# Attention scores from three digit products on two row tiles instead of plain float32, with two row buffers instead of four

## The chip, the cores and the metric

The kernel runs on one core of a Trainium2 chip. The time is the device time of one execution in microseconds (us). The kernel before takes 2467.72 us, the median of three runs (2467.32 to 2469.74).

## The reference

The input x holds 64 batch elements of 256 rows and 512 columns in float32, and adj is a 256 x 256 matrix of zeros and ones. Two layers follow each other, each with a residual and a layer norm:

```
# layer 0: attention with 8 heads of 64, masked by adj
q, k, v = x @ Wq + bq, x @ Wk + bk, x @ Wv + bv      # split into heads
scores = einsum('bqhd,bkhd->bhqk', q, k) / sqrt(64) + (1 - adj) * -1e9
out = einsum('bhqk,bkhd->bqhd', softmax(scores), v)
x = layernorm(x + out @ Wo + bo)
# layer 1
x = layernorm(x + einsum('nm,bmd->bnd', adj, x) @ weight + bias)
```

## The kernel before

The batch is worked through in 32 pairs of elements. A pair has 512 rows, so that a transposed block of its rows (xT) is a tile of 128 x 512, and every matrix product comes in blocks of 128 x 512 outputs in one PSUM bank.

**Digits.** A large product in float32 is made of three products of digits in the type F32R. `split_high` and `split_rest` (weights), `x_high` and `rest` (rows), `o_high` and `set_high` (the other left sides) cut a tile into a high digit (ScalarE, a copy with a scale to F32R), a low rest and a mixed third part `diff` (two VectorE instructions, lines 262 and 263). For weights a fourth instruction rescales the low part on ScalarE. `product` then runs 12 matmuls per block, three for each of four slices of the contraction: low, high and diff in this order (line 312). The scores are the exception: `scores` multiplies K and Q as plain float32 (line 383), 64 rows of contraction per head, with two heads at a time on the upper and lower half of the array (the two row tiles).

**Stages.** In the middle of the run each pair w takes one call of `first(w)` and one of `second(w)`, which interleave three pairs: q = w - 1, w, and n = w + 1.

- `first`: `values(q, 1)` (softmax sums and attention times V of head group 1 of the earlier pair), `scores(w, 0)`, four v blocks, q2, k2, q3, k3 of pair w (head group 1), then four o blocks (times Wo) of pair q.
- `second`: `values(w, 0)`, `scores(w, 1)`, then q0, k0, q1, k1 of the next pair n with an `adj_x` (adj times x) after each, then four l blocks (times the second layer's weight) of pair q.

Between the blocks stand the tasks of ScalarE (ACT) and VectorE (DVE). The order on PE, DVE and ACT is the order in which the program is written (`manual_schedule`), and each of these engines takes its instructions strictly in that order: one that waits holds up all behind it. Only the queues of SyncE (SP) and GpSimd (POOL) are ordered by the framework.

**What the steps below touch.**

- `scores` (lines 374 to 388) has four groups, (b, kc). Each fills two PSUM tiles of the pool `ps_at`, one per row tile, and ScalarE empties them with two Exp instructions (line 387). The pool has five buffers and `values` takes three of them just before: one for the softmax sums `zc` and two for `vc`, which ScalarE copies out (lines 343 and 356). So the sixth score tile waits for the first Exp, the seventh for the second and the eighth for the third.
- `load_x(p, i)` (lines 75 to 80) fetches block i of pair p's rows by four DMAs of 64 KB on SP's queue, in pieces of 128 bytes. `x_t` (lines 248 to 252) transposes it on DVE (line 251) and asks for the same block of the pair after: there are four buffers, so a block is asked for a whole pair ahead of its use. In `first`, `x_t(n, 0)` and `x_t(n, 1)` stand among the v blocks, `x_t(n, 2)` and `x_t(n, 3)` among the o blocks.
- The weights of a stage, 3 MB of digits, are fetched by POOL (line 114) into a ring of two stages when a stage's last block is done (`stage_end`).
- The layer norm of a pair's l result runs `mean` (DVE), `squared` (ACT, line 424), `inverse` (DVE and a power on POOL, line 430), `less` (DVE, line 435), `normed` (ACT, line 441). `with_b1` adds the bias to a residual tile (line 406, 128 x 1024 on DVE). `masked` and `summed` (lines 392 and 397) are the mask times the exponentials and their sums.
- A block's PSUM tile `mm` comes from a pool of three buffers, which are handed out in turn to blocks and `adj_x` alike.

Of the kernel before, what the change touches and what calls it, by code (L numbers as in the profile page):

```python
# [35 lines left out]
def fast(tc, x, adj, wq, bq, wk, bk, wv, bv, wo, bo, w1, b1, out):  # L36
# [34 lines left out]
    RAW, SCRATCH, W = {}, {}, {}  # L71

    def load_x(p, i):

        if p < NP:
            t = XC[p, i] = four.tile([P, D], F32, name="x")
            for q in range(4):
                nc.sync.dma_start(t[q * 32:(q + 1) * 32].rearrange("i (m j) -> i m j", j=32), xb[p, i, q])  # L80

# [79 lines left out]
    nc.gpsimd.memset(ones, 1.0)  # L161
    rows0 = []
    for i in range(4):
        t = four.tile([P, D], F32, name="o")
        nc.sync.dma_start(t, xc[0, i // 2, i % 2])
        rows0.append(t)
    for which, w in (("q", wq), ("k", wk)):
# [10 lines left out]
        nc.scalar.dma_start(RAW[which][:, :, HF:], w.rearrange("(c p) e -> p c e", p=P)[:, :, HF:])  # L178
    adj_s = two.tile([P, NC, N], F32, name="vc")
    nc.sync.dma_start(adj_s, adj.rearrange("(c p) m -> p c m", p=P))  # L180
    for i in range(4):
        load_x(1, i)
    for k in range(DC):
        if k % 2 == 0:
# [63 lines left out]
    def x_t(p, k):  # L248
        if p < NP:
            XF[p, k] = two.tile([P, D], F32, name="xT")  # L250
            nc.vector.transpose(XF[p, k], XC.pop((p, k)))
            load_x(p + 1, k)

    def x_high(p, k):
        if p < NP:
# [50 lines left out]
    def product(name, p, j):  # L306
        pm = ps_mm.tile([P, D], F32, name="mm")
        pairs = [operands(name, p, j, k) for k in range(DC)]
        n = len(pairs[0])
        for i in range(n):  # L310
            for k in range(DC):
                nc.tensor.matmul(pm, *pairs[k][i], start=i == 0 and k == 0, stop=i == n - 1 and k == DC - 1)  # L312
        scale = RHO if n == 3 else 1.0
        b, c = divmod(j, 2)
        if name in "ol":
            r = R[p][b][:, c]
            if c == 0:
                ST[p, name, b] = two.tile([P, 2], F32, name="sums")
            nc.vector.scalar_tensor_tensor(r, pm, scale, r, op0=OP.mult, op1=OP.add, accum_out=ST[p, name, b][:, c:c + 1])  # L319
        elif name == "v":  # L320
            if c == 0:
                V[p, b] = two.tile([P, NC, D], F32, name="v")
            nc.scalar.activation(V[p, b][:, c], pm, AF.Copy, scale=scale)
        else:
            T, bias = (K, bk_s) if name == "k" else (Q, bq_s)
            if c == 0:
                T[p, b] = two.tile([P, 2, 2, N], F32, name=name + "T")
            nc.scalar.activation(T[p, b][:, c].rearrange("p b i -> p (b i)"), pm, AF.Identity, bias=bias[:, j:j + 1], scale=scale)  # L328

    def values(p, g, between=()):
# [34 lines left out]
        total = acc.rearrange("p b j -> p (b j)")  # L367
        nc.gpsimd.tensor_tensor(total, total, seen, op=OP.add)
        for b in range(2):
            O[p, b, g] = four.tile([P, 2, N], F32, name="o")  # L370
            nc.vector.tensor_tensor(O[p, b, g], vc[b], rs[:, b, None].to_broadcast([P, 2, N]), op=OP.mult)

    def scores(p, g):
        if not 0 <= p < NP:
            return
        for b in range(2):
            for kc in range(NC):

                sc = [ps_at.tile([P, 2, N], F32, name="at") for s in range(2)]
                for a in range(2):  # L380
                    for s in range(2):
                        r = slice(s * HD, (s + 1) * HD)
                        nc.tensor.matmul(sc[s][:, a, :], K[p, g][r, a, b, kc * P:(kc + 1) * P], Q[p, g][r, a, b, :],  # L383
                                         start=True, stop=True)
                e = E[p, g, b, kc] = one.tile([P, 2, 2, N], F32, name=f"e{2 * b + kc}")
                for s in range(2):
                    nc.scalar.activation(e[:, s], sc[s], AF.Exp, scale=qscale)  # L387

    def masked(p, g, b, kc):
        if 0 <= p < NP:  # L390
# [8 lines left out]
    def masks(p, g, b):  # L399
        return [(masked, p, g, b, 0), (masked, p, g, b, 1), (summed, p, g, b)]  # L400
# [12 lines left out]

    def mean(p, name, b):
        if 0 <= p < NP:
            t = LN[p, name, b] = [small.tile([P, 2], F32, name=n) for n in ("mean", "squares", "rstd", "less")]
# [89 lines left out]

    def second(w, more=([], [], [])):
        q, n = w - 1, w + 1
        values(w, 0, [(squared, q, "o", 2), (squared, q, "o", 3), (hl_low, q, 0, 0), (hl_low, q, 0, 1)])
        scores(w, 1)  # L510
        masks0, masks1 = masks(w, 1, 0), masks(w, 1, 1)
        do((inverse, q, "o", 1), (with_b1, q, 0), more[0],
           (block, "q", n, 0), (less, q, "o", 1), (normed, q, "o", 2), (normed, q, "o", 3),
           (adj_x, q, 0, 0), (hl_high, q, 1, 0), (hl_low, q, 1, 0), masks0[:1], more[1],
           (block, "k", n, 0), (adj_x, q, 0, 1), (hl_high, q, 1, 1), masks0[1:2], (hl_low, q, 1, 1), masks0[2:], more[2],
           (block, "q", n, 1), (adj_x, q, 1, 0), masks1[:1],
           (block, "k", n, 1), (stage_end, n), (with_b1, q, 1), (adj_x, q, 1, 1), masks1[1:],
           (block, "l", q, 0), (block, "l", q, 1), (mean, q, "l", 0), (squared, q, "l", 0), (squared, q, "l", 1),
           (o_high, w, 0, 0), (inverse, q, "l", 0), (o_rest, w, 0, 0),
           (block, "l", q, 2), (less, q, "l", 0), (normed, q, "l", 0), (normed, q, "l", 1),  # L520
           (block, "l", q, 3), (mean, q, "l", 1), (o_high, w, 1, 0), (o_rest, w, 1, 0), (stage_end, q))
# [6 lines left out]
    def start():  # L528
        do(*((x_first, i) for i in range(4)), *((x_high, 0, i) for i in range(4)))
        v, qk1, qk0 = (pairs_of(ring_high, ring_rest, *stage) for stage in STAGES[:3])  # L530
        do((block, "q", 0, 0), (x_rest, 0, 0), (x_rest, 0, 1), v[0], (block, "k", 0, 0), (x_rest, 0, 2), v[1],
           (block, "q", 0, 1), (x_rest, 0, 3), v[2], qk1[0], (block, "k", 0, 1), (adj_t,), (square_adj,))
        scores(0, 0)
        do(qk1[1], masks(0, 0, 0), (block, "v", 0, 0), qk1[2], (x_t, 1, 0), (x_t, 1, 1),
           (block, "v", 0, 1), (x_high, 1, 0), (x_high, 1, 1), (x_rest, 1, 0), (x_rest, 1, 1), (x_t, 1, 2), (x_t, 1, 3),
           (block, "v", 0, 2), masks(0, 0, 1), (x_high, 1, 2), (x_high, 1, 3),
           (block, "v", 0, 3), (stage_end, 0), (x_rest, 1, 2), (x_rest, 1, 3),
           (block, "q", 0, 2), (block, "k", 0, 2), qk0[0], (block, "q", 0, 3), qk0[1], (block, "k", 0, 3), qk0[2],
           (stage_end, 0), (load_r, 0), (load_l,))
        values(0, 0)  # L540
        scores(0, 1)
        do((bv_wo,), (block, "q", 1, 0), masks(0, 1, 0), (block, "k", 1, 0), masks(0, 1, 1),
           (block, "q", 1, 1), (o_high, 0, 0, 0), (o_rest, 0, 0, 0),
           (block, "k", 1, 1), (stage_end, 0), (o_high, 0, 1, 0), (o_rest, 0, 1, 0))

    def last():

# [228 lines left out]
```

## Time and profile before

| what | value |
|---|---|
| median of three runs | 2467.72 us |
| time of the profiled execution | 2468.09 us |
| its span | 2466.3 us |
| PE busy | 2432.4 us (99%) |
| DVE busy | 1675.3 us (68%) |
| ACT busy | 1299.3 us (53%) |
| POOL busy | 429.7 us (17%) |
| mean granted TensorE clock | 0.996 |
| moved by DMA | 603.23 MB, 245 GB/s |

In the lines of the profile an instruction is named by line, engine, operation and tiles, as out<-in; then come the count, the busy time of the group, the mean duration in ns, and the idle time of the engine just before, with what ended it. PEld is the weight load of TensorE, which overlaps the matmul before. A float32 matmul of the program appears as two matmuls in the trace. In a timeline the first column is the start and the second the length of a run of like instructions, in us.

### The profile page before, as it was taken

The numbers are of one execution on the slowest core, as the hardware profiler recorded it, in microseconds if no ns is written. First come the engines' busy times: TensorE is split into PE (matmuls) and PEld (weight loads), VectorE is DVE, ScalarE is ACT, GpSimd is POOL, SyncE is SP. The second block draws the span as 40 slices with busy tenths as digits, with TensorE's granted clock in tenths as the row PEclk, the third lists the DMA queues.
The fourth block names the chain that finished last, engine by engine and source line by source line (L and its number), as shares of the span: only waits on it lengthen the run. The fifth ranks groups of instructions, "written<-read, shape, count | busy, mean of one in ns | idle before, by whom it ended". The sixth has DMA issues, their size and how long they took to land.

```text
span 2466.3 us, 39819 instructions
## 1 busy us (share of the span) xinstructions
PE 2432.4 (99%) x15886; PEld 1933.6 (78%) x15886; DVE 1675.3 (68%) x2807; ACT 1299.3 (53%) x2418; POOL 429.7 (17%) x720
## 2 busy tenths in 40 slices
PE   8989999999999999999999999999999999999997
PEld 6777877877878778778778787787787787877875
DVE  7766667676666766676766667666767666676665
ACT  6555454554554554545545545545455455455454
POOL 0011111111111111111111111111111111111110
PEclk9999999999999999999999999999999999999998
DMA  8868777678786687776787866878767878768650
GB/s 262 275 224 266 248 256 269 231 231 267 244 293 238 223 267 248 256 269 229 232 267 243 296 237 221 268 248 256 268 230 232 267 243 294 238 222 269 230 188 35
DMA packets 370701, 603.23 MB, mean 245 GB/s; under 512 B 272848, under 2 KB 275152, under 8 KB 310224
## 3 DMA queue, kind: packets, MB, share of 16 engines
q0 software_dynamic: 65664, 478.18, 52.1%
q1 hardware_dynamic: 302736, 120.37, 21.3%
q8 instruction: 126, 2.06, 0.3%
q10 hardware_dynamic: 2112, 2.10, 0.2%
q14 instruction: 63, 0.52, 0.1%
HBM read 551.29 MB, written 49.28 MB: 244 GB/s over the span
## 4 chain that ended last, share of the span: by engine, by line
PE 97%; DVE 2%; ACT 1%; DMA 0%; issue 0%; POOL 0%; SPq 0%; POOLq 0%; ACTq 0%; DVEq 0%
PE mm L312 71%; PE at L383 10%; PE at L353 9%; PE mm L468 5%; PE at L341 3%; DVE e L392 0%; DMA o<-in_x_dram 0%; ACT r L441 0%; DVE sl L262 0%; ACT waste L424 0%; DVE hl L458 0%; DVE sd L263 0%; PE mm L227 0%; DVE r L319 0%; DVE wr L128 0%; DVE wr L127 0%
## 5 line engine op out<-in xcount | busy, mean ns | idle before, releaser
L319 DVE SCALAR_TENSOR_TENSOR r<-mm,r 128x512 f32<-128x512 f32 x256 | 173.4, 686 | 411.4 <-PE mm L312 409.3
L392 DVE TENSOR_TENSOR e<-e,adjT 128x1024 f32<-128x1024 f32 x256 | 306.2, 1218 | 1.8 <-ACT e L387 1.7
L424 ACT ACTIVATE waste<-r,mean 128x512 bf16<-128x512 f32 x256 | 184.2, 720 | 226.7 <-DVE mean L417 222.6
L312 PE MATMUL mm<-wr,sl 128*128 128x512 f32 x1024 | 277.3, 392 | 4.0 <-DVE sl L262 4.0
L312 PE MATMUL mm<-wr,sh 128*128 128x512 f32 x1024 | 275.2, 390 | 0.0
L312 PE MATMUL mm<-wr,sd 128*128 128x512 f32 x1024 | 274.8, 390 | 0.0
L312 PE MATMUL mm<-low,wr 128*128 128x512 f32 x992 | 271.7, 395 | 0.0
L387 ACT ACTIVATE e<-at 128x512 f32<-128x512 f32 x512 | 257.6, 627 | 20.8 <-PE at L383 20.8
L312 PE MATMUL mm<-high,wr 128*128 128x512 f32 x992 | 266.3, 390 | 0.0
L312 PE MATMUL mm<-diff,wr 128*128 128x512 f32 x992 | 265.0, 389 | 0.0
L430 POOL TENSOR_TENSOR rstd<-squares,power 128x2 f32<-128x2 f32 x128 | 141.5, 1105 | 683.2 <-DVE squares L429 618.4
L441 ACT ACTIVATE r<-r,less,rstd 128x512 f32<-128x512 f32 x256 | 194.2, 807 | 117.9 <-DVE less L435 117.9
L383 PE MATMUL at<-qT,kT 64*128 64x256 f32 x2048 | 251.8, 388 | 0.6 <-ACT e L387 0.5
L383 PEld LDWEIGHTS at<-qT,kT 64*128 64x128 f32 x2048 | 210.7, 186 | 42.1 <-issue 25.7
L353 PE MATMUL at<-e,v 128*32 128x256 f32 x4096 | 232.7, 379 | 0.0
L312 PEld LDWEIGHTS mm<-wr,sl 128*128 128x128 f32 x1024 | 191.2, 189 | 43.3 <-DVE sl L262 5.0
L312 PEld LDWEIGHTS mm<-wr,sh 128*128 128x128 f32 x1024 | 193.0, 188 | 40.9
L312 PEld LDWEIGHTS mm<-wr,sd 128*128 128x128 f32 x1024 | 192.8, 188 | 40.3
L312 PEld LDWEIGHTS mm<-high,wr 128*128 128x128 f32 x992 | 186.3, 188 | 40.8
L312 PEld LDWEIGHTS mm<-diff,wr 128*128 128x128 f32 x992 | 186.2, 188 | 39.1
L328 ACT ACTIVATE qT<-mm,bq 128x512 f32<-128x512 f32 x128 | 88.1, 688 | 234.5 <-PE mm L312 234.5
L312 PEld LDWEIGHTS mm<-low,wr 128*128 128x128 f32 x992 | 177.8, 188 | 41.4 <-issue 10.1
(97 smaller groups left out, 3525.8 us busy)
## 6 DMA issues: line engine op xcount, KB each, us to landing
wr<-qk POOLq DMA_DIRECT2D x183, 1024.0 KB, 8.4
wr<-v POOLq DMA_DIRECT2D x93, 1024.0 KB, 6.7
wr<-o POOLq DMA_DIRECT2D x90, 1024.0 KB, 7.0
wr<-l POOLq DMA_DIRECT2D x90, 1024.0 KB, 8.2
r<-in_x_dram SPq DMA_DIRECT2D x32, 1024.0 KB
x<-in_x_dram SPq DMA_DIRECT2D x496, 64.0 KB
out_dram<-r SPq DMA_DIRECT2D x62, 512.0 KB
qk<-wr SPq DMA_DIRECT2D x6, 1024.0 KB
```

The source lines that it names most:

```text
L312: nc.tensor.matmul(pm, *pairs[k][i], start=i == 0 and k == 0, stop=i == n - 1 and k == DC - 1)
L319: nc.vector.scalar_tensor_tensor(r, pm, scale, r, op0=OP.mult, op1=OP.add, accum_out=ST[p, name, b][:, c:c + 1])
L328: nc.scalar.activation(T[p, b][:, c].rearrange("p b i -> p (b i)"), pm, AF.Identity, bias=bias[:, j:j + 1], scale=scale)
L341: nc.tensor.matmul(at[h * 32:(h + 1) * 32, b, :], ones, sm[:, h % 2, h // 2, :], start=True, stop=True)
L353: nc.tensor.matmul(at[h * 32:(h + 1) * 32, a, :], V[p, b][:, kc, col:col + 32], E[p, g, b, kc][:, h % 2, h // 2, :], start=kc == 0, stop=k ...
L383: nc.tensor.matmul(sc[s][:, a, :], K[p, g][r, a, b, kc * P:(kc + 1) * P], Q[p, g][r, a, b, :], start=True, stop=True)
L387: nc.scalar.activation(e[:, s], sc[s], AF.Exp, scale=qscale)
L392: nc.vector.tensor_tensor(e, e, mask[:, kc:kc + 1, :].to_broadcast([P, 4, N]), op=OP.mult)
L424: nc.scalar.activation(waste, R[p][b][:, c], AF.Square, bias=t[0][:, c:c + 1], accum_out=t[1][:, c:c + 1])
L430: nc.gpsimd.tensor_tensor(t[2], t[1], power, op=OP.pow)
L441: nc.scalar.activation(r, r, AF.Identity, scale=t[2][:, c:c + 1], bias=t[3][:, c:c + 1])
L468: nc.tensor.matmul(pm[:, j, :], t[:, i, mc, j * P:(j + 1) * P], adjT[:, mc, :], start=mc == 0 and i == 0, stop=mc == NC - 1 and i == 1)
```

## The change

The scores are computed from digits too. ScalarE writes a q or k block with its bias to a float32 tile `uncut`; `qk_high` (ACT) makes the high digit, `qk_rest` (two instructions on DVE) the low and the mixed part, and `k_low` (ACT) rescales the low part of K. `scores` then runs three F32R matmuls where one float32 matmul stood, in the order low, high, diff on the two row tiles in turn. The digits take three times the room, so K and Q have one buffer each (`one`) in place of two, the rows x have two in place of four, and the attention outputs `o` two in place of four; the four layer norm tiles become one.

With two buffers of x, `x_t(n, 0)` asks for block 2 of the same pair n, `x_t(n, 1)` for block 3, and `x_t(n, 2)` and `x_t(n, 3)` for blocks 0 and 1 of the next pair. In `second` the first masks move ahead of the q0 block, and `with_b1(q, 1)` moves from before the last `adj_x` to between the l1 block and `mean`. The start is reordered as well: two v blocks come before the first scores. The diff, cut to its core:

```diff
         if p < NP:
-            t = XC[p, i] = four.tile([P, D], F32, name="x")
+            t = XC[p, i] = two.tile([P, D], F32, name="x")
...
-    for i in range(4):
+    for i in range(2):
         load_x(1, i)
...
             nc.vector.transpose(XF[p, k], XC.pop((p, k)))
-            load_x(p + 1, k)
+            load_x(p + k // 2, (k + 2) % DC)
...
             if c == 0:
-                T[p, b] = two.tile([P, 2, 2, N], F32, name=name + "T")
-            nc.scalar.activation(T[p, b][:, c].rearrange("p b i -> p (b i)"), pm, AF.Identity, bias=bias[:, j:j + 1], scale=scale)
+                T[p, b] = one.tile([P, 2, 3, D], F32R, name=name + "T")
+            UNCUT[name, p, j] = two.tile([P, D], F32, name="uncut")
+            nc.scalar.activation(UNCUT[name, p, j], pm, AF.Identity, bias=bias[:, j:j + 1], scale=scale)
+
+    def qk_high(name, p, j):
+        if 0 <= p < NP:
+            t = (K if name == "k" else Q)[p, j // 2][:, j % 2]
+            nc.scalar.activation(t[:, 0], UNCUT[name, p, j], AF.Copy, scale=CUT)
+
+    def qk_rest(name, p, j):
+
+        if 0 <= p < NP:
+            t = (K if name == "k" else Q)[p, j // 2][:, j % 2]
+            high, low, diff = (t[:, i] for i in range(3))
+            nc.vector.scalar_tensor_tensor(low, high.bitcast(F32), -RHO, UNCUT.pop((name, p, j)), op0=OP.mult, op1=OP.add)
+            if name == "q":
+                nc.vector.scalar_tensor_tensor(diff, low.bitcast(F32), -FINE, high.bitcast(F32), op0=OP.mult, op1=OP.add)
+            else:
+                nc.vector.scalar_tensor_tensor(diff, high.bitcast(F32), -1 / FINE, low.bitcast(F32), op0=OP.mult, op1=OP.add)
+
+    def k_low(p, j):
+        if 0 <= p < NP:
+            low = K[p, j // 2][:, j % 2, 1]
+            nc.scalar.activation(low, low.bitcast(F32), AF.Copy, scale=FINE / RHO)
...
-            O[p, b, g] = four.tile([P, 2, N], F32, name="o")
+            O[p, b, g] = two.tile([P, 2, N], F32, name="o")
...
                 for a in range(2):
-                    for s in range(2):
-                        r = slice(s * HD, (s + 1) * HD)
-                        nc.tensor.matmul(sc[s][:, a, :], K[p, g][r, a, b, kc * P:(kc + 1) * P], Q[p, g][r, a, b, :],
-                                         start=True, stop=True)
+                    for i in (1, 0, 2):
+                        for s in range(2):
+                            r = slice(s * HD, (s + 1) * HD)
+                            nc.tensor.matmul(sc[s][:, a, :], K[p, g][r, a, i, keys], Q[p, g][r, a, i, b * N:(b + 1) * N],
+                                             start=i == 1, stop=i == 2)
...
-           (block, "q", w, 2), (block, "k", w, 2), more[1], (block, "q", w, 3), more[2], (block, "k", w, 3), (stage_end, w),
-           (x_high, n, 0), (x_high, n, 1),
-           (block, "o", q, 0), (x_rest, n, 0), (x_t, n, 2), (x_high, n, 2),
+           (block, "q", w, 2), (qk_high, "q", w, 2), (qk_rest, "q", w, 2),
+           (block, "k", w, 2), (qk_high, "k", w, 2), (qk_rest, "k", w, 2), more[1],
+           (block, "q", w, 3), (k_low, w, 2), (qk_high, "q", w, 3), (qk_rest, "q", w, 3), more[2],
+           (block, "k", w, 3), (stage_end, w), (qk_high, "k", w, 3), (qk_rest, "k", w, 3), (x_high, n, 0), (x_high, n, 1),
+           (block, "o", q, 0), (k_low, w, 3), (x_rest, n, 0), (x_t, n, 2), (x_high, n, 2),
...
+        masks1 = masks(w, 1, 1)
+        do((inverse, q, "o", 1), (with_b1, q, 0), masks(w, 1, 0), more[0],
+           (block, "q", n, 0), (less, q, "o", 1), (normed, q, "o", 2), (normed, q, "o", 3), masks1[:1],
+           (adj_x, q, 0, 0), (hl_high, q, 1, 0), (hl_low, q, 1, 0), masks1[1:2], more[1],
+           (block, "k", n, 0), (adj_x, q, 0, 1), (hl_high, q, 1, 1), (hl_low, q, 1, 1),
+           (qk_high, "q", n, 0), (qk_rest, "q", n, 0), (qk_high, "k", n, 0), (qk_rest, "k", n, 0), more[2],
+           (block, "q", n, 1), (k_low, n, 0), (adj_x, q, 1, 0), (qk_high, "q", n, 1), masks1[2:],
+           (block, "k", n, 1), (stage_end, n), (adj_x, q, 1, 1), (qk_high, "k", n, 1), (qk_rest, "q", n, 1),
+           (block, "l", q, 0), (qk_rest, "k", n, 1), (k_low, n, 1), (block, "l", q, 1), (with_b1, q, 1),
+           (mean, q, "l", 0), (squared, q, "l", 0), (squared, q, "l", 1),
            (o_high, w, 0, 0), (inverse, q, "l", 0), (o_rest, w, 0, 0),
```

More of the change, by code (lines that the diff above doesn't have):

```diff
@@ L70, in fast @@
     XC, XF, XP, R, Q, K, V, E, SM, O, SET, HL, ST, LN = ({} for _ in range(14))
-    RAW, SCRATCH, W = {}, {}, {}
+    RAW, SCRATCH, W, UNCUT = {}, {}, {}, {}
     def load_x(p, i):
         if p < NP:
-            t = XC[p, i] = four.tile([P, D], F32, name="x")
+            t = XC[p, i] = two.tile([P, D], F32, name="x")
             for q in range(4):
@@ L163, in fast @@
     for i in range(4):
-        t = four.tile([P, D], F32, name="o")
+        t = four.tile([P, D], F32, name="low")
         nc.sync.dma_start(t, xc[0, i // 2, i % 2])
@@ L379, in scores @@
                 sc = [ps_at.tile([P, 2, N], F32, name="at") for s in range(2)]
+                keys = slice(b * N + kc * P, b * N + (kc + 1) * P)
                 for a in range(2):
-                    for s in range(2):
-                        r = slice(s * HD, (s + 1) * HD)
-                        nc.tensor.matmul(sc[s][:, a, :], K[p, g][r, a, b, kc * P:(kc + 1) * P], Q[p, g][r, a, b, :],
-                                         start=True, stop=True)
+                    for i in (1, 0, 2):
[3 more added lines that the diff above has]
+                                             start=i == 1, stop=i == 2)
                 e = E[p, g, b, kc] = one.tile([P, 2, 2, N], F32, name=f"e{2 * b + kc}")
                 for s in range(2):
-                    nc.scalar.activation(e[:, s], sc[s], AF.Exp, scale=qscale)
+                    nc.scalar.activation(e[:, s], sc[s], AF.Exp, scale=RHO * qscale)
     def masked(p, g, b, kc):
@@ L415, in mean @@
         if 0 <= p < NP:
-            t = LN[p, name, b] = [small.tile([P, 2], F32, name=n) for n in ("mean", "squares", "rstd", "less")]
+            ln = small.tile([P, 4, 2], F32, name="ln")
+            t = LN[p, name, b] = [ln[:, i] for i in range(4)]
             nc.vector.tensor_scalar(t[0], ST.pop((p, name, b)), -1 / D, None, op0=OP.mult)
@@ L510, in second @@
         scores(w, 1)
[L511 to L518, printed above, removed]
+        masks1 = masks(w, 1, 1)
[8 more added lines that the diff above has]
+           (mean, q, "l", 0), (squared, q, "l", 0), (squared, q, "l", 1),
            (o_high, w, 0, 0), (inverse, q, "l", 0), (o_rest, w, 0, 0),
@@ L530, in start @@
         v, qk1, qk0 = (pairs_of(ring_high, ring_rest, *stage) for stage in STAGES[:3])
-        do((block, "q", 0, 0), (x_rest, 0, 0), (x_rest, 0, 1), v[0], (block, "k", 0, 0), (x_rest, 0, 2), v[1],
-           (block, "q", 0, 1), (x_rest, 0, 3), v[2], qk1[0], (block, "k", 0, 1), (adj_t,), (square_adj,))
-        scores(0, 0)
[L534 to L538, printed above, removed]
+        do((block, "q", 0, 0), (qk_high, "q", 0, 0), (x_rest, 0, 0), (x_rest, 0, 1), v[0],
+           (block, "k", 0, 0), (qk_high, "k", 0, 0), (x_rest, 0, 2), (x_rest, 0, 3), v[1],
+           (block, "q", 0, 1), (qk_high, "q", 0, 1), v[2], (block, "k", 0, 1), (qk_high, "k", 0, 1), (adj_t,),
+           (qk_rest, "k", 0, 0), (k_low, 0, 0), (qk_rest, "q", 0, 0), (qk_rest, "k", 0, 1), (k_low, 0, 1), (qk_rest, "q", 0, 1),
+           qk1[0], (block, "v", 0, 0), qk1[1], (block, "v", 0, 1))
+        scores(0, 0)
+        do(qk1[2], (square_adj,), masks(0, 0, 0), (x_t, 1, 0), (x_t, 1, 1),
+           (block, "v", 0, 2), (x_high, 1, 0), (x_high, 1, 1), masks(0, 0, 1),
+           (block, "v", 0, 3), (stage_end, 0), (x_rest, 1, 0), (x_rest, 1, 1), (x_t, 1, 2), (x_t, 1, 3),
+           (block, "q", 0, 2), (qk_high, "q", 0, 2), qk0[0],
+           (block, "k", 0, 2), (qk_high, "k", 0, 2), (qk_rest, "q", 0, 2), (qk_rest, "k", 0, 2), (k_low, 0, 2), qk0[1],
+           (block, "q", 0, 3), (qk_high, "q", 0, 3), (x_high, 1, 2), (x_high, 1, 3), qk0[2],
+           (block, "k", 0, 3), (qk_high, "k", 0, 3), (qk_rest, "q", 0, 3), (qk_rest, "k", 0, 3), (k_low, 0, 3),
            (stage_end, 0), (load_r, 0), (load_l,))
@@ L541, in start @@
         scores(0, 1)
-        do((bv_wo,), (block, "q", 1, 0), masks(0, 1, 0), (block, "k", 1, 0), masks(0, 1, 1),
-           (block, "q", 1, 1), (o_high, 0, 0, 0), (o_rest, 0, 0, 0),
-           (block, "k", 1, 1), (stage_end, 0), (o_high, 0, 1, 0), (o_rest, 0, 1, 0))
+        qk0 = [(f, name, 1, j) for j in range(2) for name in "qk" for f in (qk_high, qk_rest)]
+        do((bv_wo,), (x_rest, 1, 2), (x_rest, 1, 3), (block, "q", 1, 0), masks(0, 1, 0), qk0[:2],
+           (block, "k", 1, 0), qk0[2:4], (k_low, 1, 0), masks(0, 1, 1),
+           (block, "q", 1, 1), qk0[4:6], (o_high, 0, 0, 0), (o_rest, 0, 0, 0),
+           (block, "k", 1, 1), qk0[6:], (k_low, 1, 1), (stage_end, 0), (o_high, 0, 1, 0), (o_rest, 0, 1, 0))
     def last():
```

## The prediction

> **What bounds the kernel now.** I read the page's busy shares first, then the chain that ended last, then the groups, and last the timelines of one pair of batches. The page:
>
> ```profile
> PE 2432.4 (99%) x15886; PEld 1933.6 (78%) x15886; DVE 1675.3 (68%) x2807; ACT 1299.3 (53%) x2418; POOL 429.7 (17%) x720
> ...
> PE 97%; DVE 2%; ACT 1%; DMA 0%; issue 0%; POOL 0%; SPq 0%; POOLq 0%; ACTq 0%; DVEq 0%
> PE mm L312 71%; PE at L383 10%; PE at L353 9%; PE mm L468 5%; PE at L341 3%; DVE e L392 0%; DMA o<-in_x_dram 0%; ACT r L441 0%; DVE sl L262 0%; ACT waste L424 0%; DVE hl L458 0%; DVE sd L263 0%; PE mm L227 0%; DVE r L319 0%; DVE wr L128 0%; DVE wr L127 0%
> ...
> L387 ACT ACTIVATE e<-at 128x512 f32<-128x512 f32 x512 | 257.6, 627 | 20.8 <-PE at L383 20.8
> ```
>
> TensorE is the whole chain; the scores (L383) are a tenth of it. A tenth can shrink, but any new wait of PE lengthens the end one for one. So the question is how late ACT and DVE may be. TensorE's timeline of one `adj_x`, and of the scores and what follows:
>
> ```profile
> 1203.55 1.11 PE L468 MATMUL mm<-adjT,hl 128*128 128x256 f32 x8
> 1204.49 1.09 PE L312 MATMUL mm<-wr,sl 128*128 128x512 f32 x4
> ...
> 1219.96 3.92 PE L383 MATMUL at<-qT,kT 64*128 64x256 f32 x32
> 1223.81 1.20 PE L312 MATMUL mm<-wr,low 128*128 128x512 f32 x4
> ```
>
> A scores call takes 3.85 us from its start to the next block's; 64 calls are 246 us. ScalarE around the same call, then around the next one:
>
> ```profile
> 1218.99 0.72 ACT L424 ACTIVATE waste<-r,mean 128x512 bf16<-128x512 f32 x1
> 1219.62 0.19 ACT L424 ACTIVATION_READ_ACCUMULATOR waste<-r,mean 128x1 f32 x1
> 1219.72 1.06 ACT L356 ACTIVATE vc<-at 128x512 f32<-128x512 f32 x2
> 1221.12 4.03 ACT L387 ACTIVATE e<-at 128x512 f32<-128x512 f32 x8 [0.34 <-PE at L383]
> ```
>
> ```profile
> 1256.28 1.52 ACT L441 ACTIVATE r<-r,less,rstd 128x512 f32<-128x512 f32 x2 [1.43 <-DVE less L435]
> 1257.83 1.15 ACT L453 ACTIVATE hl<-r 128x512 fp32r<-128x512 f32 x2
> ...
> 1260.92 1.06 ACT L356 ACTIVATE vc<-at 128x512 f32<-128x512 f32 x2
> 1262.29 1.09 ACT L387 ACTIVATE e<-at 128x512 f32<-128x512 f32 x2 [0.30 <-PE at L383]
> ```
>
> ACT is 53% busy, yet it stands idle only 0.34 and 0.30 us before the first Exp: a queue that comes a microsecond late into a scores call holds TensorE. VectorE and SP in `first`:
>
> ```profile
> 1250.56 0.70 DVE L251 STREAM_TRANSPOSE xT<-x 128x512 f32<-128x512 f32 x1
> ...
> 1253.48 0.70 DVE L251 STREAM_TRANSPOSE xT<-x 128x512 f32<-128x512 f32 x1
> 1254.11 0.12 DVE L429 TENSOR_SCALAR squares<-squares 128x2 f32<-128x2 f32 x1
> ...
> 1256.09 0.15 DVE L435 TENSOR_TENSOR less<-mean,rstd 128x2 f32<-128x2 f32 x1
> ```
>
> ```profile
> 1235.07 0.34 SPq L80 DMA_DIRECT2D x<-in_x_dram  x1
> 1235.51 0.58 SPq L85 DMA_DIRECT2D r<-in_x_dram  x1
> 1236.15 18.09 SPq L80 DMA_DIRECT2D x<-in_x_dram  x8
> ```
>
> The last view matters most: the DMAs asked for by the first two transposes (1234.3 and 1235.0) keep SP issuing until 1253.7.
>
> **The change, part by part.**
>
> *1. The scores themselves, 64 calls.* Two rows bear on F32R with 256 columns: `adj_x` runs eight in 0.94 us, 0.117 each; the float32 score pairs start every 0.216, their two halves 7 ns apart, so the two row tiles load and multiply side by side. I take 0.117 per pair: 24 pairs and a first weight load of 0.10 (spacing of the first two loads) are 2.9 us. But ACT binds first. The first Exp can start 0.10 + 6 x 0.117 + 0.2 (from the last matmul to the Exp) = 1.0 after the start, where it was 1.16. Exps start 0.477 apart and the third lasts 0.605; it must end before the eighth score tile starts: 1.0 + 0.95 + 0.6 + 0.05 (semaphore) + 0.10 (weight load) + 6 x 0.117 = 3.42, against 3.76 before (last pair 3.54 + 0.216). So 0.34 saved per call, **-22 us** in all. Ends: no gate by Exp, 0.85 each, -54; row tiles in F32R one after the other, 48 x 0.117 = 5.6, +1.9 each, +120.
>
> The Trainium skill (TensorE: Matmul & The Clock Gate, The mechanism) says that weight loads overlap running matmuls only where the row group differs. By that a pair would cost a load of 0.107 (its 128 columns at 1.2 per ns, an estimate from the section LDWEIGHTS) and then 0.107 of matmul, 5.2 us a call, 1.8 more than by the row. The `adj_x` row speaks against it: each of its eight matmuls has a new 128-column load in the same row group and still follows after 0.117.
>
> *2. Blocks 2 and 3 of x, now asked for in the stage that needs them.* Today they lie in SBUF a whole pair ahead. After, `x_t(n, 0)` at 1234.3 asks for block 2 and `x_t(n, 1)` for block 3; SP passes them no other entry than now (out and r stand where they stood), and the number of DMAs is the same. So they get the slot that today's loads of (n+1, 0) and (n+1, 1) have. In the trace's DMA packets those have all arrived at 1247.3 and 1256.3: the 128-byte pieces go at 50 to 66 per us while POOL's weight loads (1235 to 1243, 1247 to 1254) run, and up to 1300 per us between. Block 2 is due on DVE at 1250.56: 3 us in hand. Block 3 is due at 1253.48: **2.8 us late**. Ten other pairs show 2.3 to 3.1 and one 5.1. Due times and weight loads hang on the same block ends, so a later PE shifts both.
>
> DVE stops there; behind it stand `squares`, the o2 residual, `less`; behind `less` on ACT the two `normed`, `hl`, `zc`, `squared`, `vc`, and the Exps of `scores(w, 1)`. The only slack is the 0.30 above, less 0.16 as the first Exp is wanted earlier. PE loses about 2.55 in each of 30 calls: **+76 us**. Ends: 0 (it lands in time) and 5 a call.
>
> *3. Digits of q and k.* Per pair 8 `qk_high` and 4 `k_low` on ACT (0.52 apart, as `x_high`) are 6.2 us; 8 `qk_rest` of 0.72 + 0.61 on DVE (L262 after L263) are 10.6. ACT's Identity stays (0.585). In `first` the half of it falls where DVE idles 13.0 us (before the o0 residual at 1248.62), and the last rest ends 0.2 before that residual: cost 0; without that cover it would push the o blocks by up to 5.3. In `second` DVE had 9.4 us idle and gets 5.3, but in places: counted from the start of the q0 block (S = 1189.6 in the trace), masks fill the idle 5.4; the rest of `adj_x(0, 1)` runs 8.7 to 10.0, hl to 10.6, q0's digits to 11.9, k0's to 13.2. `k_low(n, 0)` stands on ACT ahead of the digits of `adj_x(1, 0)` and waits for it: 13.3, so their high digit comes at 13.85 instead of 11.2 and the low one at 14.5 to 15.2. That frees the PSUM buffer that l0 needs at 14.65: PE waits 0.67, 30 times, **+20 us**. Ends: 0, if ACT and DVE are 0.6 faster, and 1.5 if they are 0.8 slower.
>
> *4. The layer norm of l.* DVE goes on: sums to 17.0, rest of `adj_x(1, 1)` to 18.4, q1's digits to 19.7, l0 residual, k1's digits to 21.65, l1 residual at 21.65 where it was 20.85. Then `with_b1` (1.135) now stands before `mean`. So `mean`, `squared`, `less`, `normed`, `o_high`, `zc`, `squared`, `vc` all come 0.8 + 1.1 = 1.9 later: ACT is free for the first Exp at S + 33.0, not 31.1. PE's scores start at 30.1 + 0.67 and want it 1.0 later, 31.75. PE waits 1.26, 30 times, **+38 us**. Ends: 0 and 2.5.
>
> *5. The start.* DVE is nearly full from 13.6 to 60 us (idle some 5 us) and gets 8 rests, 10.6 us; blocks 2 and 3 of pair 1 must be fetched in the midst, where such loads took 11 to 15 us, and the digits of q and k stand behind their transposes. **+10**, ends 4 and 25. The buffers of `o`, K, Q and `uncut` are each free when asked for, but for q1's `uncut` (0.9 late, hidden: its PSUM buffer is next needed 1.7 later): 0; PSUM buffers beyond these would show as PE waits at L312.
>
> Sum: -22 + 76 + 20 + 38 + 10 = +122 on the profiled execution's 2468.1 (span 2466.3 and 1.8 around it), which is 0.4 above the median: **2590 us**, 5% slower.
>
> **Rivals.** *Block 3 is not late* (its packets find room before the second weight load). For it: the page's queues take 74% of the DMA engines, so there is room somewhere; against: twelve pairs of twelve. Then part 2 is 0: 2514, still slower by parts 3 and 4.
>
> *Everything new is covered; this one ends faster.* Place: the ACT queue at the first Exp; if the chain into it is late by no more than 0.3 us in both halves, parts 2 to 4 are 0 and only the saving counts: 2446, or 2414 if Exps don't gate either. For it: mean shares of 68% and 53%, which leave 24 and 35 us of a pair's 75.4 idle. Against: the idle time is not where the work goes. It decides at 0.3 us of lateness; I find 2.8 and 1.9.
>
> *The F32R row tiles don't run side by side.* No row shows them. At 0.234 per pair a call takes 5.7 us instead of 3.42; the late Exps then hide some of their lateness, and about 3.1 more per pair stay: 2590 + 94 = 2685. The change then doesn't do what it says. For: no F32R in tiles in this trace; against: float32 does it at 7 ns.
>
> **How the numbers follow.** Likeliest, 0.69: parts 1 to 5 as summed, 2590, own range 2545 to 2640 (lateness 2.3 to 3.5, parts 3 and 4 each off by half). Block 3 in time: 0.11, 2514. All covered: 0.10, 2446. Tiles in turn: 0.08, 2685. The rest, 0.02, near no change. The range 2500 to 2650 takes the likeliest and the first rival, leaving out 2 in 10. About 0.2% (5 us) is what a measurement of this kernel can tell from no change. Faster 0.11, same 0.02, slower 0.87.
>
> **What the profile after would show.** Part 1: 48 score matmuls a call, pairs 0.117 apart until the sixth tile. Part 2: DVE idle before the transposes (L251), ended by DMA of x, near 84 us in 30 waits. Part 3: ACT idle before `k_low` on DVE, PE idle before `l` blocks. Part 4: no idle of ACT before the Exps, PE's weight loads for scores waiting for ACT, some 110 us in all; PE's share falls to about 94%. I am wrong if the DMA wait is absent, if ACT still idles before the Exps, or if the pairs stand 0.2 or more apart.

## The result, and the profile after

The changed kernel takes 2736.72 us (median of four runs, 2732.40 to 2740.01) against 2468.73 of the kernel before beside it: 1.1083 times as long, with an interval of 1.1064 to 1.1102. That is 268 us more. The forecast was 122 more, with 2650 as the upper end of its range, so the direction was right and the size was not.

The page of the changed kernel, busy shares, the chain that ended last, and two groups (busy time, mean ns of one, then the idle time ahead of them and its releaser):

```profile
PE 2508.9 (92%) x16910; PEld 1990.6 (73%) x16910; DVE 2016.4 (74%) x3319; ACT 1513.2 (55%) x2802; POOL 429.0 (16%) x720
...
DVE 36%; PE 19%; ACT 16%; DMA 12%; SPq 10%; issue 2%; DVEq 0%; POOL 0%; POOLq 0%; ACTq 0%
...
L407 PE MATMUL at<-qT,kT 64*128 64x256 f32 x3072 | 302.4, 338 | 172.9 <-ACT zc L365 101.9
...
L251 DVE STREAM_TRANSPOSE xT<-x 128x512 f32<-128x512 f32 x124 | 84.0, 697 | 175.1 <-DMA x<-in_x_dram 175.1
```

TensorE was 97% of the chain and is now 19% of it. The chain runs through SP's queue, the loads of x, and VectorE. The last two lines belong together: VectorE loses 175 us to the loads of x, and TensorE loses 173 in the scores. VectorE around the transposes of blocks 2 and 3 (start, length, and in brackets what the engine waited for), and SP's queue in the same pair:

```profile
1305.72 0.69 DVE L263 SCALAR_TENSOR_TENSOR diff<-low,high 128x512 fp32r<-128x512 f32 x1
1308.44 0.71 DVE L251 STREAM_TRANSPOSE xT<-x 128x512 f32<-128x512 f32 x1 [2.03 <-DMA x<-in_x_dram]
...
1310.58 0.69 DVE L263 SCALAR_TENSOR_TENSOR diff<-low,high 128x512 fp32r<-128x512 f32 x1
1315.39 0.71 DVE L251 STREAM_TRANSPOSE xT<-x 128x512 f32<-128x512 f32 x1 [4.12 <-DMA x<-in_x_dram]
1316.03 0.13 DVE L454 TENSOR_SCALAR ln<-ln 128x2 f32<-128x2 f32 x1
```

```profile
1291.43 0.34 SPq L80 DMA_DIRECT2D x<-in_x_dram  x1
1291.86 0.51 SPq L85 DMA_DIRECT2D r<-in_x_dram  x1
1292.43 26.31 SPq L80 DMA_DIRECT2D x<-in_x_dram  x15
```

Here VectorE stands 2.0 and then 4.1 us. Next ScalarE, which waits behind the `ln` of 1316.03 (`inverse`) and the later `less`, and TensorE in the call `scores(w, 1)` that follows:

```profile
1318.19 1.52 ACT L466 ACTIVATE r<-r,ln 128x512 f32<-128x512 f32 x2 [1.42 <-DVE ln L460]
1319.74 1.15 ACT L478 ACTIVATE hl<-r 128x512 fp32r<-128x512 f32 x2
1320.80 0.58 ACT L365 ACTIVATE zc<-at 128x512 f32<-128x512 f32 x1
...
1322.83 1.06 ACT L378 ACTIVATE vc<-at 128x512 f32<-128x512 f32 x2
1323.79 2.24 ACT L411 ACTIVATE e<-at 128x512 f32<-128x512 f32 x4
```

```profile
1316.89 0.98 PE L407 MATMUL at<-qT,kT 64*128 64x256 f32 x12
1321.43 0.58 PE L407 MATMUL at<-qT,kT 64*128 64x256 f32 x1 [3.56 <-ACT zc L365]
1323.46 3.87 PE L407 MATMUL at<-qT,kT 64*128 64x256 f32 x35 [1.45 <-ACT vc L378]
1327.26 1.19 PE L312 MATMUL mm<-low,wr 128*128 128x512 f32 x4
```

TensorE fills two score tiles, then waits for the PSUM tiles that ScalarE's `zc` and `vc` copies free. The call takes 10.37 us to the next block, where 3.85 stood before. This is the path that the forecast described, with a longer wait at its head. The 35 matmuls at the end are new: in the call of the other head group, where the wait is short, the same 35 take 2.92 us, not 3.87:

```profile
1358.16 1.09 PE L407 MATMUL at<-qT,kT 64*128 64x256 f32 x13
1359.82 2.92 PE L407 MATMUL at<-qT,kT 64*128 64x256 f32 x35 [0.57 <-ACT vc L378]
1362.67 1.19 PE L312 MATMUL mm<-wr,low 128*128 128x512 f32 x4
```

The view by stretches gives the reason (busy time of each engine, then the granted clock, the DMA share and GB/s):

```profile
1278.00:1317.00 39.00, 39.00 (x249) 30.79 (x247) 25.66 (x41) 18.14 (x33) 5.55 (x9) 1.00 0.84 254
1317.00:1321.40 4.40, 0.87 (x12) 0.66 (x12) 4.18 (x10) 3.17 (x6) 1.55 (x3) 0.84 0.81 245
1321.40:1325.40 4.00, 2.52 (x19) 2.23 (x21) 3.83 (x8) 3.89 (x9) 0.61 (x2) 0.50 1.44 369
1325.40:1327.20 1.80, 1.80 (x21) 1.72 (x19) 1.80 (x3) 1.61 (x4) 1.77 (x2) 0.61 1.46 404
1327.20:1358.00 30.80, 30.53 (x211) 24.30 (x208) 23.65 (x40) 16.58 (x31) 3.97 (x7) 1.00 0.45 153
```

The clock falls to half within the wait of 3.56 us (0.81 is the mean of that stretch), is 0.50 for most of the 35 matmuls, and comes back as the call ends. The prediction has no such term.

The stretch from one scores call to the next, in the median pair, is used for all that follows: from `scores(w, 0)` to `scores(w, 1)` and on to the next `scores(w, 0)` it was 41.17 and 34.21 us before. After it is 41.83 and 41.35.

### The profile page after: what moved, and what is told of

Read it like the earlier page. It is cut to its first block, busy times and chain, and to the rows that moved or that the text cites. A ratio compares the mean times of both kernels' runs of the same rounds, so it can differ in the third digit from the quotient of the medians.

```text
span 2730.6 us, 42849 instructions
## 1 busy us (share of the span) xinstructions
PE 2508.9 (92%) x16910; PEld 1990.6 (73%) x16910; DVE 2016.4 (74%) x3319; ACT 1513.2 (55%) x2802; POOL 429.0 (16%) x720
## 4 chain that ended last, share of the span: by engine, by line
DVE 36%; PE 19%; ACT 16%; DMA 12%; SPq 10%; issue 2%; DVEq 0%; POOL 0%; POOLq 0%; ACTq 0%
PE mm L312 12%; DMA x<-in_x_dram 12%; SPq L80 10%; PE at L407 6%; DVE sd L263 5%; ACT r L466 5%; DVE sl L262 5%; DVE e L416 4%; ACT waste L449 4%; DVE r L430 3%; DVE r L319 3%; ACT sh L276 2%; DVE sm L421 2%; DVE kT L345 2%; DVE qT L343 2%
## 5 line engine op out<-in xcount | busy, mean ns | idle before, releaser
L407 PE MATMUL at<-qT,kT 64*128 64x256 f32 x3072 | 302.4, 338 | 172.9 <-ACT zc L365 101.9
L407 PEld LDWEIGHTS at<-qT,kT 64*128 64x128 f32 x3072 | 254.0, 232 | 232.9 <-ACT zc L365 108.0
L312 PE MATMUL mm<-wr,sl 128*128 128x512 f32 x1024 | 281.8, 396 | 19.1 <-DVE sl L262 8.9
L312 PE MATMUL mm<-low,wr 128*128 128x512 f32 x992 | 280.7, 406 | 1.7 <-DVE low L262 1.7
L411 ACT ACTIVATE e<-at 128x512 f32<-128x512 f32 x512 | 265.6, 615 | 11.8 <-PE at L407 9.6
L466 ACT ACTIVATE r<-r,ln 128x512 f32<-128x512 f32 x256 | 194.2, 806 | 117.5 <-DVE ln L460 116.1
L455 POOL TENSOR_TENSOR ln<-ln,power 128x2 f32<-128x2 f32 x128 | 142.2, 1111 | 597.0 <-DVE ln L454 534.8
L329 ACT ACTIVATE uncut<-mm,bq 128x512 f32<-128x512 f32 x128 | 88.0, 687 | 238.0 <-PE mm L312 186.7
L449 ACT ACTIVATE waste<-r,ln 128x512 bf16<-128x512 f32 x256 | 184.2, 719 | 60.8 <-DVE ln L442 56.5
L312 PEld LDWEIGHTS mm<-low,wr 128*128 128x128 f32 x992 | 183.9, 195 | 40.4 <-issue 4.0
L251 DVE STREAM_TRANSPOSE xT<-x 128x512 f32<-128x512 f32 x124 | 84.0, 697 | 175.1 <-DMA x<-in_x_dram 175.1
```

The costliest lines, as they stand in the source:

```text
L329: nc.scalar.activation(UNCUT[name, p, j], pm, AF.Identity, bias=bias[:, j:j + 1], scale=scale)
L407: nc.tensor.matmul(sc[s][:, a, :], K[p, g][r, a, i, keys], Q[p, g][r, a, i, b * N:(b + 1) * N], start=i == 1, stop=i == 2)
L411: nc.scalar.activation(e[:, s], sc[s], AF.Exp, scale=RHO * qscale)
L449: nc.scalar.activation(waste, R[p][b][:, c], AF.Square, bias=t[0][:, c:c + 1], accum_out=t[1][:, c:c + 1])
L455: nc.gpsimd.tensor_tensor(t[2], t[1], power, op=OP.pow)
L466: nc.scalar.activation(r, r, AF.Identity, scale=t[2][:, c:c + 1], bias=t[3][:, c:c + 1])
```

## The experiments

### The two buffers of x alone

`x_two_alone` is the kernel before with nothing but the late loads:

```diff
-            t = XC[p, i] = four.tile([P, D], F32, name="x")
+            t = XC[p, i] = two.tile([P, D], F32, name="x")
...
-    for i in range(4):
+    for i in range(2):
...
-            load_x(p + 1, k)
+            load_x(p + k // 2, (k + 2) % DC)
```

> The kernel before with only the rows changed: two buffers of x, blocks 2 and 3 asked for by the transposes of blocks 0 and 1 of the same pair; scores stay float32, no digits of q and k. Late rows (theory): VectorE waits for the DMA some 6 us per pair (2.0 before block 2, 4.1 before block 3, as in the changed kernel), ScalarE has 0.3 us in hand, so TensorE loses about 5.8 us per pair and, as its clock falls to half behind such a wait, some 0.7 more: 2468 + 30 x 6.5 = 2663 us. Digits (rival): the rows are worth at most the 2.55 us per pair of the prediction, 2545 us or less, and the larger part of the 268 us is the digits' work.

Measured: 2694.89 us against 2468.0 before, a ratio of 1.0918 (1.0896 to 1.0940). Its line of waits:

```profile
DVE xT L251 <- DMA x<-in_x_dram: 184.6, 35, 8.7
```

The late loads cost 227 us by themselves, without a digit in the scores; the second stretch of a pair goes from 34.21 to 41.2. The rival falls. So does the size that the prediction gave: a pair loses 7, where it counted 2.55. The theory's own sum, 2663, is 32 us short as well: 10.5 us are lost before the third scores call, which it left out, and a pair loses 7.1 in the mean where it took 6.5.

### The late loads taken out of the changed kernel

`x_rows` keeps two buffers and the same requests but fetches whole rows of 2 KB in place of 128-byte pieces (block i then holds its rows in another arrangement). `x_four` has four buffers again and asks a pair ahead; to make room, `uncut` lies in the buffers of `vc` (four of the first blocks in those of `diff`). `uncut_in_vc` makes that second edit alone.

```diff
-            t = XC[p, i] = two.tile([P, D], F32, name="x")
+            t = XC[p, i] = four.tile([P, D], F32, name="x")
...
-            load_x(p + k // 2, (k + 2) % DC)
+            load_x(p + 1, k)
...
-            UNCUT[name, p, j] = two.tile([P, D], F32, name="uncut")
+            UNCUT[name, p, j] = four.tile([P, D], F32, name="diff") if p == 0 and j < 2 else two.tile([P, D], F32, name="vc")
```

> The changed kernel with the same four DMAs of 64 KB per block of x, but each partition takes one whole row of 2 KB in place of 16 pieces of 128 bytes; the rows then stand in another order, so the output is not the reference's. Late rows, because small pieces get few turns beside the weight loads (theory): the wait of the transposes falls from 175 us to under 20, and 2468 + 30 x 1.3 (parts 3 and 4 less part 1) + 10 for the start = 2515 us. If what delays the loads is their place in SP's queue and not the size of the pieces: the wait stays over 100 us, over 2650 us.

> The changed kernel with four buffers of x again and each block asked for a pair ahead, as before; the room comes from uncut, which takes the buffers of vc (and of diff for the first four blocks). Late rows (theory): no wait for x, 2515 us (2500 to 2530), with the scores of first still 0.6 us longer than before by ScalarE's lateness. Digits (rival): over 2650 us.

> Control for the run with four buffers of x: the changed kernel with uncut in the buffers of vc alone, two buffers of x. Both theories: within 10 us of the changed kernel, 2727 to 2747 us, with some 175 us of waits for x.

Measured: `x_rows` 2525.55 us (ratio 1.0232, 1.0212 to 1.0253), 10 above the figure expected, `x_four` 2520.94 (1.0212, 1.0195 to 1.0229), `uncut_in_vc` 2733.44 in a single run. At the transposes VectorE waits for x 3.8 us in all in `x_rows` and not at all in `x_four`, and the place of `uncut` costs nothing that a single run shows. `x_rows` leaves every request in its place in SP's queue, so the rival about that place falls: from the same place, rows of 2 KB are in time and pieces of 128 bytes are not. Two different ways of having x in time agree: the late x is worth 2736.7 - 2520.9 = 216 us, and all the rest of the change 52. The page of `x_four` (busy shares, chain):

```profile
PE 2448.7 (97%) x16910; PEld 1937.2 (77%) x16910; DVE 2014.7 (80%) x3319; ACT 1509.7 (60%) x2802; POOL 430.8 (17%) x720
...
PE 57%; DVE 23%; ACT 13%; issue 1%; DMA 1%; POOL 0%; POOLq 0%; DVEq 0%; ACTq 0%; SPq 0%
```

Its median pair has stretches of 41.84 and 34.47, 0.94 more than before. Its trace shows where: `scores(w, 0)` waits 0.5 to 0.6 for `vc` and takes 4.51, that is 0.96 more than the 3.55 of `scores(w, 1)`, where no wait is left; and l0 comes 0.58 late. The start shows 15.6 us more until the third scores call, and in pair 1 the first stretch takes 51.42 in place of 41.84. The 9.6 us are lost at o0, where TensorE waits 6.2 us in all for ScalarE (the digits of Wo, L129) and then runs at a granted clock of 0.50 from 128.5 to 133 us.

### Digits in other places of the queues, and another start

`order` is `x_four` with two tasks moved, neither added nor removed. `start` is `order` with the first pair left in plain float32 scores and the kernel before's order of tasks up to its second scores call, and the digits of Wo made ahead of those of q and k in pair 1.

```diff
-           (block, "q", n, 1), (k_low, n, 0), (adj_x, q, 1, 0), (qk_high, "q", n, 1), masks1[2:],
+           (block, "q", n, 1), (adj_x, q, 1, 0), (k_low, n, 0), (qk_high, "q", n, 1), masks1[2:],
...
-           (block, "l", q, 0), (qk_rest, "k", n, 1), (k_low, n, 1), (block, "l", q, 1), (with_b1, q, 1),
-           (mean, q, "l", 0), (squared, q, "l", 0), (squared, q, "l", 1),
+           (block, "l", q, 0), (qk_rest, "k", n, 1), (k_low, n, 1), (block, "l", q, 1),
+           (mean, q, "l", 0), (squared, q, "l", 0), (squared, q, "l", 1), (with_b1, q, 1),
```

> The kernel with four buffers of x, and two tasks moved in the queues: with_b1(q, 1) behind the two squared (into VectorE's wait for their sums) and k_low(n, 0) behind the digits of adj_x(1, 0). Nothing is added or left out. Theory (parts 3 and 4: the two waits come from the places of these two tasks, not from engines that are too full): the wait of 0.97 in each scores(w, 0) and that of 0.58 before each l0 go, a pair becomes 0.62 shorter than before instead of 0.94 longer (the trace of the kernel with four buffers, median pair), 30 x 1.56 = 47 less than its 2521: 2474, 2465 to 2485; the start's 27 us stay. Rival (VectorE and ScalarE are full in `second`, and a task that is moved only hands its lateness on): 2505 to 2525, with PE still waiting in scores(w, 0) or now before l2.

> The kernel `order` with the first pair of batches left in plain float32 (its queries and keys go without digits, as in the kernel before) and the digits of Wo made ahead of those of q2, k2 and q3 in pair 1. Theory (the rest of the loss is the start: 15.6 until the third scores call from digits in the full queues of the start, and one wait of 9.6 before o0 of pair 1, where the digits of Wo stand behind those of q and k): 2474 - 25 = 2449, 2440 to 2460, faster than the kernel before. Rival (the start waits for its loads and weights whatever the queues do): 2465 to 2480, the same as `order`, no faster than before.

Measured: `order` 2477.43 us (ratio 1.0037, 1.0024 to 1.0051), `start` 2456.91 (0.9952, 0.9939 to 0.9966). Moving two tasks gives back 43.5 us. The median pair of `order` has stretches of 40.87 and 33.90, so both waits are gone, 0.97 and 0.58, and a pair is 0.61 shorter than before. TensorE's timeline of `order` in `scores(w, 0)`:

```profile
1162.50 3.62 PE L407 MATMUL at<-qT,kT 64*128 64x256 f32 x48
1166.05 1.19 PE L312 MATMUL mm<-wr,low 128*128 128x512 f32 x4
```

The rival (engines too full) falls: DVE has as many instructions as in `x_four` and is busier (82% of the span, 80% there), but it is 2% of the chain that ended last, where it was 23%. `start`, which has digits in the scores from the second pair on, recovers 20.5 of the 26 us of the start and beats both kernels, the one before by 0.5%. Its third scores call comes 14.8 us sooner than in `order`, and the first stretch of pair 1 is 8.7 shorter. Its page shows TensorE as before, with VectorE at 82%:

```profile
PE 2418.3 (99%) x16878; PEld 1926.1 (78%) x16878; DVE 2009.0 (82%) x3303; ACT 1507.9 (61%) x2790; POOL 446.0 (18%) x720
```

### The score products by themselves

`mm_alone` is the kernel before with three F32R products of the same K and Q, so that TensorE does the new work and the other engines the old:

```diff
-                T[p, b] = two.tile([P, 2, 2, N], F32, name=name + "T")
+                T[p, b] = two.tile([P, 2, 2, N], F32R, name=name + "T")
...
+                    for i in range(3):
...
-                                         start=True, stop=True)
+                                             start=i == 0, stop=i == 2)
...
-                    nc.scalar.activation(e[:, s], sc[s], AF.Exp, scale=qscale)
+                    nc.scalar.activation(e[:, s], sc[s], AF.Exp, scale=qscale / 3)
```

> The kernel before with each float32 score product replaced by three F32R products of the same operands, added up, and the scale of Exp divided by three: the digits are left out, so the output is not the reference's; what is left is part 1 by itself, with x in its four buffers and both queues as before. Theory (part 1: pairs 0.117 apart, the call gated by its Exps): 64 x -0.34 = -22, 2446, 2438 to 2452. Rival a (no gate by Exp): 2414. Rival b (row tiles in turn): 2560 or more. Rival c (a shorter call only lets TensorE run ahead into a wait elsewhere): 2460 to 2470.

Measured: 2448.61 us, a ratio of 0.9919 (0.9904 to 0.9934), 20.0 us less than before. A call takes 3.55 us from its start to the next block in place of 3.85. The gain of part 1 is real, and with all else in time it is what the change brings. `start` lies 8.3 us above it: by the traces, 2.8 of that is pair 1, and 5.1 comes after the last `scores(w, 0)`.

### The clock

`warm` is the changed kernel with useless matmuls where TensorE waits in any case:

```diff
         values(w, 0, [(squared, q, "o", 2), (squared, q, "o", 3), (hl_low, q, 0, 0), (hl_low, q, 0, 1)])
+        idle = ps_mm.tile([P, D], F32, name="mm")
+        for i in range(IDLE):
+            nc.tensor.matmul(idle, adjT[:, 0, 0:P], adjT.rearrange("p c n -> p (c n)"), start=i == 0, stop=i == IDLE - 1)
         scores(w, 1)
```

> The changed kernel with 22 useless F32R matmuls (adjT by adjT, 512 columns, 0.227 each, 5.0 us) ahead of scores(w, 1), where TensorE waits 5.5 us or more in all but the first pair; the late x stays as it is. Theory (the halved clock after a wait of some 3.6 us costs about 1 us of each call: 35 matmuls in 3.87 instead of 2.92): with the wait filled the clock stays at 1.0, 2737 - 29 x 1 + 5 = 2713, 2700 to 2725. Rival (the clock is a mark in the profile, the call ends with the late Exps whatever it is): 2735 to 2750.

Measured: 2699.45 us (two runs), at the lower end of the range given and 37 less than the changed kernel; between the two profiled spans it is 31.5. TensorE's timeline, and the same place by stretches:

```profile
1388.51 5.28 PE L541 MATMUL mm<-adjT 128*128 128x512 f32 x22
1393.72 1.08 PE L409 MATMUL at<-qT,kT 64*128 64x256 f32 x13
1395.05 2.92 PE L409 MATMUL at<-qT,kT 64*128 64x256 f32 x35 [0.25 <-ACT vc L380]
```

```profile
1393.60:1398.00 4.40, 4.15 (x50) 3.30 (x49) 4.23 (x8) 4.37 (x11) 1.63 (x2) 1.00 1.37 390
```

More work on TensorE makes the kernel shorter. The clock stays at 1.00 here, and the 35 matmuls take 2.92 us again, although x is as late as it was (VectorE waits 177.2 us for it, 175.1 without the useless matmuls). So 1.0 to 1.2 us of each of 30 calls, on average, is the halved clock, not the wait. The Trainium skill (TensorE: Matmul & The Clock Gate, Part 1: The HAM clock gate) says that the clock falls to half after an idle window of about 3.4 us; the wait of 3.56 us and the 0.50 shown above agree.

The length of that one wait is no threshold, though. In the changed kernel's trace 29 calls of `scores(w, 1)` have such a first wait, of 2.28 to 5.90 us, each followed by a second one of 1.45 to 1.65; in all 29 the clock is at 0.50 for a part of the call, and 15 of the first waits are shorter than 3.4 us. The 0.57 in `scores(w, 0)` doesn't bring it down.

### One late block in place of two

`three` puts a formula for the lateness to the test on `start`: with three buffers only block 3 is asked for in the stage that needs it, from where block 2 was asked for.

```diff
-            load_x(p + 1, k)
+            if p > 1:
+                load_x(p + (k + 3) // 4, (k + 3) % 4)
+            elif k < 3:
+                load_x(2, k)
```

> The kernel `start` with three buffers of x in place of four: from pair 2 on only block 3 is asked for in the stage that needs it, and one transpose earlier than in the changed kernel (by x_t(n, 0), in the place that block 2 has there); block 3 of pair 1 is loaded ahead in a `diff` buffer. Theory (the lateness is arrival of the last packet after the asking transpose, plus about 2.5 until VectorE goes on, less the time at which the block is due): 13.1 + 2.5 = 15.6 against a due time of 18.6, 3 us in hand, no wait of VectorE for x in nearly all pairs: 2457, 2450 to 2465. Rival (any block asked for beside POOL's weight loads comes too late, whichever it is): waits of 1 to 5 us for x in block 3 of most pairs, and 2490 to 2600.

Measured: 2469.75 us (ten runs, 2460.47 to 2475.41), a ratio of 1.0000 (0.9987 to 1.0014). That is 13 us above `start` and 5 above the range given. The waits:

```profile
DVE xT L252 <- DMA x<-in_x_dram: 12.3, 4, 4.6
```

The rival falls, as most pairs have no wait. Block 3 is in time in all but four pairs, but those four cost TensorE 1.0, 3.5, 5.4 and 5.7 us, together as much as the 15.3 us between the two profiled spans.

When a block is whole can be read from its landing marks. Each of a block's four DMAs leaves sixteen marks in the trace, updates of a semaphore on which the transpose waits. In the trace of the changed kernel the 34 transposes that wait for x start 0.02 to 0.5 us after the last of the block's 64 marks, 0.12 in the median. In `three` the block is due 19.1 us after the transpose that asks for it. From pair 3 on, half of each DMA's marks are there after 13.1 to 14.1 us in every pair, also in the four late ones. In these four the last mark comes only after 20.3 to 23.6 us; in all other pairs it is there after 19.0 or less. So a few of the sixteen parts of a DMA come late, not the block as a whole, and a margin against the median is not a margin against the scatter. Why these parts come late is not shown.

## Why the prediction was wrong

| part | predicted | measured | from |
|---|---|---|---|
| 1, the scores | -22 | -20 | `mm_alone` less before |
| 2, blocks 2 and 3 of x | +76 | +216 | changed less `x_four` |
| 3, `k_low` and l0 | +20 | +17 | 0.57 a pair, trace of `x_four` |
| 4, layer norm of l | +38 | +29 | 0.96 a pair, trace of `x_four` |
| 5, the start | +10 | +26 | 15.6, 9.6 in pair 1 and 1 at the end, trace of `x_four` |
| sum | +122 | +268 | |

**Part 2 is the step that failed, by its size: +76 forecast, +216 measured.** Its mechanism stood as written: SP keeps issuing, the pieces come slowly beside POOL's weight loads, VectorE stops at L251, and the queue behind it makes the Exps late. What failed is the reading of when a block has landed, "those have all arrived at 1247.3 and 1256.3", and with it "3 us in hand" for block 2 and "2.8 us late" for block 3.

A block is 2048 pieces, and in the order in which pieces of x land, the 2048th of the second load comes at 1256.2. But SP issues the next block before this one is whole, so that count can mix the two, and a few parts lag behind the rest. By the landing marks of the same trace the two loads are whole at 1249.4 and 1258.4. That is 1.1 us in hand and 4.9 us late. Over 26 pairs of that trace the slot of block 3 is 5.5 us late in the median (3.4 to 12.7), and the slot of block 2 is missed in six.

The trace of the changed kernel shows the same. After `x_t(n, 0)`, the 2048th piece of block 3 comes at 22.2 us (median), where the forecast has 22.0, but the last mark at 24.3. The block is due at 18.6, 0.5 sooner than in the trace of before. So it is 5.7 late, and VectorE waits 5.0 for it in the median pair, 5.5 where block 2 was in time. Block 2 is due at 15.6 and whole at 14.5 in the median, but after 16.4 to 24.1 in 9 of 30 pairs, and there it takes the wait over in whole or in part. Together it is 5.8 a pair (175 us in 30 pairs). A small slip lies in the sum too: 2.8 less a slack of 0.30 - 0.16 is 2.66 a call, not 2.55, or 3 us in all.

The other part of the miss is the price of a late microsecond. I passed lateness on to TensorE one for one. Of the 7.2 us that a pair loses (216 in 30), 1.0 to 1.2 are the clock, for which the sum has no term. It was missing at the lateness that I forecast too: in the changed kernel's trace a first wait of 2.28 us was enough, with the second of 1.65 behind it. My upper end for this part, 5 a call, was set by one pair of twelve and not by the unknown in the method.

**Part 1 was right**, and so was the reading that ACT binds first. In the trace of the changed kernel the two row tiles start 3 to 4 ns apart and pairs follow after about 0.12 us, which rules out the rival of tiles in turn. The call is 3.55 against 3.42 + 0.10 by my walk.

**Parts 3 and 4 were right in place and cause**; their sizes are 0.1 and 0.3 a pair too large. `order` moves exactly the two tasks named there and takes both waits away. It moves them in one run, so that each wait belongs to its task rests on the traces: the scores stretch loses 0.97 and the l stretch 0.58.

**Part 5 was too small, for a reason I could have had.** I bounded it by VectorE's idle time before the third scores call. I didn't walk pair 1, where the digits of Wo share the queues with those of q and k: in `x_four`, o0 comes 9.6 us late there, behind ScalarE, and in `start`, with those digits made earlier, that stretch is 9.1 us shorter.

Of the signs named in advance, VectorE's wait was to be 84 us and is 175.1; TensorE's share was to be 94% and is 92%; the weight loads of the scores were to wait about 110 us for ACT and wait 108.0 for `zc` and 77.3 for `vc`. The first rival (block 3 in time) is what `x_four` has in effect: 2521, where I gave 2514. The faster rival (2446) is what `start` comes near to, with the digits in other places and none in the first pair: the gain appears when nothing else is late, as `mm_alone` shows with its 20 us.

## What to carry to other kernels

A load is in time when the last of its parts has landed. Read that moment from the landing marks on which the waiting instruction depends, not from a count of packets, and compare the margin with the scatter of arrivals, not with their median. On the engine that bounds a kernel, price a wait twice: a wait of 2.3 us with a second one close behind it halved the clock here, and that slowed the matmuls after it. And where an added task fits an engine's share but not its queue, look at what stands behind it first: here two tasks moved by a few places were worth 43.5 us.

## What the runs showed that I had not expected

- A kernel that waits can be made faster with useless matmuls: 22 of them in each pair took 31 to 37 us off 2737, as the clock stayed up.
- The sixteen parts of one DMA don't land together. In the nine pairs in which block 2 is late in the changed kernel, its last mark comes 4.4 us (median) after half of each DMA's marks are there.
- Block loads in pieces of 128 bytes, at the same place of the loop, are whole 13.5 to 23.6 us after the transpose that asks for them in `three` (from pair 3 on), and its runs differ by 15 us, where those of `start` differ by 3.
